# A two-layer kernel's list planner: new step prices, a serial pair and another set of due times for the recurrent layer

## The chip, the core and the metric

The kernel runs on one core of a Trainium2 chip, as one program. The metric is the device time of that program in microseconds (us); a profile of one execution gives a span, from the first to the last instruction, and the order and length of every instruction on the five engines: PE (TensorE matmuls; PEld is its weight loads), DVE (VectorE), ACT (ScalarE), POOL (GpSimd) and SP (SyncE, which here issues the DMAs).

## What is computed

Batch 32, 128 tokens, width 512, all in float32. Layer 0 is a cross-attention block with 32 query heads and 8 key/value heads, followed by a layer norm. Layer 1 is a recurrent block. The change touches only layer 1:

```python
xn = _ln(x, ln1_w, ln1_b)
sx = _token_shift(xn, state[:, i1])
xxx = tanh((xn + sx * maa_x) @ maa_w1).reshape(b, l, 5, 1, 32)
xxx = matmul(xxx, maa_w2).reshape(b, l, 5, E)
x5 = xn[:, :, None] + sx[:, :, None] * (maa_stack + xxx)
w = exp(-exp(time_decay + tanh(x5[:, :, 1] @ decay_w1) @ decay_w2))
r = x5[:, :, 3] @ Wr.T;  k = x5[:, :, 0] @ Wk.T;  v = x5[:, :, 2] @ Wv.T
g = silu(x5[:, :, 4] @ Wg.T)
def step(s, rkvw):                     # 32 heads of 16 x 16 state, 128 steps
    a = k_t[:, :, :, None] * v_t[:, :, None, :]
    out = einsum('bhk,bhkd->bhd', r_t, u * a + s)
    return a + w_t[:, :, :, None] * s, out
att = group_norm(outs) * gn_w + gn_b
x = x + (att * g) @ Wo.T
xn2 = _ln(x, ln2_w, ln2_b); sx2 = _token_shift(xn2, state[:, i0])
rr = sigmoid((xn2 + sx2 * ffn_maa_r) @ ffn_Wr.T)
kk = square(relu((xn2 + sx2 * ffn_maa_k) @ ffn_Wk.T))
x = x + rr * (kk @ ffn_Wv.T)
```

## The kernel before

The 32 sequences go in 16 groups of two, so that a tile of one group has 128 partitions (features) and 256 columns (two sequences of 128 tokens); the width of 512 is four such chunks `c`. For each group layer 1 has three parts.

`front` makes, from the layer norm and the shift (`xn`, `sx`), the five mixed inputs `x5` (a small matmul into a PSUM tile `px`, a DVE operation that takes it in, a POOL addition), then the projections `pk`, `pv`, `pr`, `pg` on PE, their copies or activations on ACT, the product `rk` of r and k on DVE (L742 in the profile; the copy of r from the same PSUM tile is L734 on ACT), the gate `gt` (L761 on ACT, L771 on DVE), and the decay exponents `ew`. v is stored to DRAM (`vd`) so that it can be fetched back spread over partitions.

`recurrence` runs, for each chunk and each quarter `dd`, the state update as a scan along time: SP fetches `kv` (eight DMAs of 128 KB for two quarters, L1316), ACT fills the first column, POOL multiplies by k (L1339), DVE scans (L1355) into the PSUM tile `a`, multiplies by r (L1370), and PE sums over the state (`acc`, L1386). PE also computes `pd` (the term with u, from `rk`) and `pc` (centred outputs).

`tail` normalizes (`pvar`, `rstd`, `pb`), applies the gate, projects (`pwo`), adds to x (`x1c`), and runs the feed-forward part (`pkk`, `pkv`, `prr`), and writes the result. Its two weights `fk` and `fr` (1 MB each) are loaded for every group into one buffer.

None of these steps is written out in program order. Each is handed to a planner by `add`, with its engine, a price in us (`work`), the tiles that it reads and writes, and a due time; the planner (`give_out`) then plays a list schedule and writes out the instructions in the order of that play, so that each engine's queue is fixed when the kernel is built. Layer 0 and the first half of `front` for group 0 are planned by one `Plan`, the rest of layer 1 by a second one (`pl1`). On the chip the engines then run their queues in order and wait for each other by semaphores; a price changes nothing but the order.

The due time of a step is its group's number plus an entry of the table `WHEN0` or `WHEN1`, named by engine and tile. `_turns` first pulls every due time down to just below the earliest one among the steps that depend on it, and sets the order in which the tiles of a tag take their buffers. In `give_out` each engine takes, among its ready steps, the one that could start without delay (under 0.3 us) with the smallest due time:

```python
if s.eng != "SP" and s.due > line[first].due + self.ahead:
    continue
at = free[e]
for s0 in s.before:
    at = max(at, s0.end + (0.0 if s0.eng == e else self.AFTER[s0.eng]))
```

`ahead` is the lookahead in groups: no step may be taken that is due later than the earliest unfinished one by more than that. `AFTER` is the time from one engine's end to another's start. `mode` is the shape in which a PE step uses the array ("full", "rows" for `px`, `pew` and `pb`, "cols" for `acc`, `pdd` and `pvar`, "turn" for transposes); a step in another mode than the one before it costs `SWITCH` more. Prices are formulas: `mm(n, times, share)` for PE, 0.215 us for a pass of 256 columns; `dve(n)` = 0.14 + 1.06 n/1000; `pool_(n)` = 0.08 + 2.3 n/1000; some are literal (2.3 for the scan, 0.48 for the operation at `px`). A fetch of `kv` takes 6.0 us of the wire in the plan, and 3.0 us until it has landed.

Small PSUM tiles share the tag "g" with three buffers; it is exempt from the order of turns (`FREE`). `a` and `acc` have one buffer each in PSUM, `kv` and `ar` three in SBUF.

Of the kernel before, what the change touches and what calls it, by code (L numbers as in the profile page):

```python
# [30 lines left out]
SWITCH = 0.17  # L31
# [43 lines left out]
}  # L75
WHEN1 = {
    "ACT": """
        att 0: 0.4337, att 1: 0.2346, att 2: 0.4481, att 3: 42.2036, ew 0: 11.1338, ew 1: -0.2147, ew 2: 26.1389,
        ew 3: -0.1243, gt 0: 26.2110, gt 2: 2.1890, h0: 0.5241, hd: 0.3002, kk 0: 0.9228, kk 2: 20.4292,
        kv 0 0 0: 25.5890, kv 0 0 1: 21.9376, kv 0 1 0: 6.0558, kv 0 1 1: 0.8322, kv 1 0 0: 6.3560, kv 1 0 1: 29.3594,  # L80
        kv 1 1 0: 9.2616, kv 1 1 1: 25.6198, kv 2 0 0: 43.5542, kv 2 0 1: 7.4919, kv 2 1 0: 8.5948, kv 2 1 1: 43.5152,
        kv 3 0 0: 9.4194, kv 3 0 1: 22.4588, kv 3 1 0: 30.1517, kv 3 1 1: 12.4171, pk 0: 26.3643, pk 2: 24.3430,
        pv 0: 22.5942, pv 2: -0.1385, r 0: 26.3795, r 2: 23.3115, rr 0: 40.0790, rr 1: 27.6728, rstd: 26.0489,
        sq 0: -0.1128, sq 1: 23.3775, sq 2: 36.1033, sq 3: 41.1479, w4 0: 25.5550, w4 1: 21.3052, w4 2: 2.5964,
        w4 3: 27.6773, xnc 0: 8.8046, xnc 1: 1.2163, xnc 2: 4.5961, xnc 3: 10.3705, xnt 0: 37.5160, xnt 1: 36.3160,
        xnt 2: -1.1905, xnt 3: 3.6365, xx 0: 20.5242, xx 1: 34.9847, xx 2: 23.3521, xx 3: 22.4330, yk 0: 41.2808,
        yk 1: 20.7056, yk 2: 23.1054, yk 3: 23.1512, yr 0: 42.3101, yr 1: 3.1488, yr 2: 21.3085, yr 3: 2.7447,
        zc 0: 0.7541, zc 1: 27.0647, zt 0: 0.2936, zt 1: 22.7466
    """,
    "DVE": """  # L90
        a 0 0: 23.1285, a 0 1: 44.6967, a 0 2: 19.4777, a 0 3: 17.2122, a 1 0: 22.0121, a 1 1: 24.8715, a 1 2: 8.6631,
        a 1 3: 9.3222, a 2 0: 23.2268, a 2 1: 8.2943, a 2 2: 21.2763, a 2 3: 8.0300, a 3 0: 1.3330, a 3 1: 44.9810,
        a 3 2: 36.5134, a 3 3: 42.7805, ar 0 0: 1.0179, ar 0 1: 22.3833, ar 0 2: 27.7052, ar 0 3: 25.6817,
        ar 1 0: 37.2615, ar 1 1: 13.6436, ar 1 2: 22.7659, ar 1 3: 45.7511, ar 2 0: 6.0171, ar 2 1: 12.5578,
        ar 2 2: 28.8789, ar 2 3: 15.8516, ar 3 0: 23.3130, ar 3 1: 23.1491, ar 3 2: 19.9556, ar 3 3: 32.9812,
        gn 0: 23.7852, gn 1: 20.9580, gn 2: 33.5535, gn 3: 46.4228, gt 0: -0.0231, gt 2: -0.1977, own 0: 5.1099,
        own 1: 0.1224, own 2: -0.0283, own 3: 0.3349, pb 0: 8.0751, pb 1: 2.2968, pb 2: 0.8375, pb 3: 20.4024,
        raw 0: 23.2010, raw 1: 3.5965, raw 2: 23.2455, raw 3: 44.4584, rk 0: -0.7509, rk 1: -0.1719, rr 0: 1.6746,
        rr 1: 1.3382, rstd: 7.6463, st c 0: 11.1186, st c 1: 40.4898, st t 0: 28.5724, st t 1: 15.0321, x1c 0: 2.5303,
        x1c 1: 26.0962, x5 0 0: 2.7039, x5 0 1: 2.7955, x5 0 2: 24.3069, x5 0 3: 21.8074, x5 1 0: -0.0972,  # L100
        x5 1 1: 21.6197, x5 1 2: 0.6004, x5 1 3: 22.4358, x5 2 0: 42.1808, x5 2 1: -0.8591, x5 2 2: 41.2059,
        x5 2 3: 37.6158, x5 3 0: 26.8334, x5 3 1: 24.0914, x5 3 2: 23.6554, x5 3 3: 2.4313, x5 4 0: 25.8630,
        x5 4 1: 22.1314, x5 4 2: 40.0832, x5 4 3: 41.0197
    """,
    "PE": """
        acc 0: 22.3033, acc 1: 7.0581, acc 2: 22.7806, acc 3: 4.9952, pb 0: 27.7390, pb 2: 22.7260, pc 0: 2.0619,
        pc 1: 28.1521, pc 2: 3.1673, pc 3: 23.4917, pd 0: 33.6053, pd 1: 24.8921, pd 2: 20.8375, pd 3: 23.9500,
        pdd: -1.1093, pew 0: 23.8627, pew 2: 5.8633, pg 0: 23.5794, pg 2: 22.0824, ph0: -0.4813, pk 0: -1.0989,
        pk 2: -0.6925, pkk 0: 19.1077, pkk 2: 22.4386, pkv 0: 19.0064, pkv 1: 23.2658, pr 0: 1.2036, pr 2: 2.3445,
        prr 0: 1.8637, prr 1: 21.7968, pv 0: -0.8518, pv 2: 7.2890, pvar: 5.4151, pwo 0: 32.7897, pwo 1: 23.4460,  # L110
        px5 1 0: 39.8845, px5 1 2: 11.2421, px5 2 0: 23.4434, px5 2 2: 23.3758, px5 4 0: 0.9353, pxnc 0: 24.0019,
        pxnc 2: 21.6438, pxnt 0: -1.1522, pxnt 2: 13.7523
    """,
    "POOL": """
        kv 0 0 0: 26.0772, kv 0 0 1: 23.5502, kv 0 1 0: 27.7860, kv 0 1 1: 29.1526, kv 1 0 0: 0.4056,
        kv 1 0 1: 25.8430, kv 1 1 0: 5.7684, kv 1 1 1: 31.4921, kv 2 0 0: 28.2020, kv 2 0 1: 19.5485,
        kv 2 1 0: 29.7046, kv 2 1 1: 42.4003, kv 3 0 0: 10.6540, kv 3 0 1: 4.0853, kv 3 1 0: 25.5882,
        kv 3 1 1: 22.5557, rr 0: 2.4732, rr 1: 44.9550, sd c 0: 18.3198, sd c 1: 13.1243, sd t 0: 33.5214,
        sd t 1: 22.7124, sxc 0: 2.6017, sxc 2: 21.1060, sxt 0: 21.9776, sxt 2: -1.3154, x5 0 0: 41.1636,
        x5 0 2: 2.6161, x5 1 0: 34.2012, x5 1 2: 22.9652, x5 2 0: 22.8432, x5 2 2: 24.0895, x5 3 0: 23.6407,  # L120
        x5 3 2: 27.8090, x5 4 0: 41.2196, x5 4 2: 26.2718, xx 0: 24.1836, xx 2: 9.4476, yk 0: 24.7724, yk 2: 33.3339,
        yr 0: 1.5862, yr 2: 3.3642
    """,
    "SP": """
        fk: 43.5334, fr: 16.5653, kv 0 0 0: 26.7655, kv 0 1 0: 23.9392, kv 1 0 0: 24.5017, kv 1 1 0: 4.2079,
        kv 2 0 0: 5.4685, kv 2 1 0: 28.7358, kv 3 0 0: 28.1974, kv 3 1 0: 22.0650, rr 0: 3.0366, rr 1: 1.8101,
        s0 0: -0.6787, s0 1: 24.2956, vd 0: 11.0274, vd 1: 0.8056, vd 2: -0.1035, vd 3: 13.7197, x1c 0: 41.2264,
        x1c 1: 2.1599, x1t 0: 23.3682, x1t 1: 35.1410
    """,
}  # L130

# [29 lines left out]
class Plan:  # L161
# [6 lines left out]
    def __init__(self, ctx, tc, when, ahead):  # L168
# [6 lines left out]
                self.when[f"{eng} {name.strip()}"] = float(at)  # L175
        self.pools, self.steps, self.begun, self.turns = {}, [], {}, True

    def tag(self, name, bufs, space=None):
        kw = {} if space is None else {"space": space}
        pool = self.ctx.enter_context(self.tc.tile_pool(name=name, bufs=bufs, **kw))  # L180
        self.pools[name] = (pool, bufs, [])
# [66 lines left out]
    def give_out(self):  # L248
# [95 lines left out]
def xattn_rwkv_kernel(  # L344
# [263 lines left out]
    def front(g, D):  # L608
# [120 lines left out]
        for c in range(0, KC, 2):  # L729
# [5 lines left out]
                r=[pp],  # L735
# [894 lines left out]
```

## Time and profile before

| | us |
|---|---|
| median of 3 runs (lowest, highest) | 2126.89 (2120.77, 2129.71) |
| the profiled execution | 2124.67 |
| its span | 2122.9 |

| engine | busy us | share of the span | instructions |
|---|---|---|---|
| PE | 1975.3 | 93% | 11908 |
| PEld | 1280.5 | 60% | 11908 |
| DVE | 1787.5 | 84% | 2182 |
| ACT | 1048.4 | 49% | 3473 |
| POOL | 1294.3 | 61% | 1081 |

The granted clock of PE over the span is 0.975 on average. A float32 matmul is recorded as two instructions. Matmuls overlap in the records: one of 256 columns has a mean of some 385 ns, while sixteen in a row take 3.65 us; the busy time of PE counts overlapping ones once. Layer 0 ends at about 640 us, the first scan of layer 1 starts at 691 us, and the last ends at 2062.7 us. The columns of every view are named where lines are shown; "idle" is the time in which the engine stood just before an instruction, with what ended it. The kernel's instructions are in a helper's line in some cases (L546 for all projections, L564 for those by token), and the tile's name tells them apart.

### The profile page before, as it was taken

To read this page: it belongs to the slowest core of one execution; us is meant where nothing else is said; L and a number is where in the kernel's file an instruction comes from. 1 tells how busy PE (TensorE), PEld (TensorE's weight loads), DVE (VectorE), ACT (ScalarE), POOL (GpSimd) and SP (SyncE) were. 2 spreads that over 40 slices of the span, in tenths; PEclk is the share of its full clock that TensorE was granted. 3 is DMA by queue.
4 is the path that set the end of the run, shared out by engine and by line. 5 is a ranking of instruction groups with operands and counts; after the bars stand their busy time and mean duration, and the time that the engine had idled before them with its cause. 6 is when DMAs were issued, how large, how long until landed. Compare 5 with 4: busy or idle time off the path is not lost.

```text
span 2122.9 us, 36158 instructions
## 1 busy us (share of the span) xinstructions
PE 1975.3 (93%) x11908; PEld 1280.5 (60%) x11908; DVE 1787.5 (84%) x2182; ACT 1048.4 (49%) x3473; POOL 1294.3 (61%) x1081
## 2 busy tenths in 40 slices
PE   6989999999988689999999999999999999999976
PEld 5656666666656356666566665665656656566533
DVE  3878898988872899989889898998988989989881
ACT  4867888888872133443334434344343443433332
POOL 1363342424245767878678786777867868778652
PEclk9999999999999799999999999999999999999997
DMA  7232222222114887887879879798797887978870
GB/s 203 71 115 63 65 66 65 61 69 62 41 41 91 127 123 124 151 161 125 158 129 152 160 123 162 130 152 161 118 167 127 150 165 120 164 139 128 158 133 30
DMA packets 155947, 252.23 MB, mean 119 GB/s; under 512 B 50576, under 2 KB 97712, under 8 KB 139376
## 3 DMA queue, kind: packets, MB, share of 16 engines
q1 hardware_dynamic: 151136, 242.31, 62.4%
q10 hardware_dynamic: 4624, 7.63, 1.1%
q8 instruction: 94, 1.54, 0.4%
q14 instruction: 93, 0.76, 0.2%
HBM read 224.12 MB, written 25.69 MB: 118 GB/s over the span
## 4 chain that ended last, share of the span: by engine, by line
PE 31%; DMA 16%; DVE 11%; SPq 5%; issue 1%; ACT 1%; POOL 0%; DVEq 0%; POOLq 0%; ACTq 0%
DMA kv<-vd 16%; PE pk L546 5%; PE pkk L546 5%; DVE a L1355 5%; SPq L721 3%; PE pwo L564 3%; PE px L637 3%; PE acc L1386 3%; PE pg L546 2%; DVE ar L1370 2%; PE pv L546 2%; PE pkv L564 2%; SPq L1316 2%; PE pdd L705 1%; PE ph L532 1%
## 5 line engine op out<-in xcount | busy, mean ns | idle before, releaser
L1339 POOL TENSOR_TENSOR kv<-kv,kx 128x1016 f32<-128x1016 f32 x256 | 597.5, 2351 | 164.8 <-DMA kv<-vd 118.7
L1355 DVE TENSOR_TENSOR_SCAN a<-w,kv 128x1024 f32<-128x1024 f32 x256 | 586.7, 2292 | 15.3 <-ACT kv L1329 2.9
L1062 ACT ACTIVATE pr<-pr,mx 128x128 f32<-128x128 f32 x1024 | 396.1, 391 | 51.0 <-DVE mx L1049 38.5
L1370 DVE TENSOR_TENSOR ar<-a,r 128x1024 f32<-128x1024 f32 x256 | 312.4, 1220 | 8.4 <-DVE a L1355 0.5
L668 POOL TENSOR_TENSOR x<-x,xnt 128x512 f32<-128x512 f32 x160 | 186.5, 1184 | 71.0 <-DVE x L653 70.8
L1062 ACT ACTIVATION_READ_ACCUMULATOR pr<-pr,mx 128x1 f32 x1024 | 194.3, 190 | 0.0
L1036 DVE TENSOR_TENSOR pr<-sc,m 128x1024 f32<-128x1024 f32 x128 | 155.9, 1218 | 28.7 <-PE sc L1020 25.0
L1074 PE MATMUL ppT<-ident,pr 128*128 128x128 f32 x1024 | 154.7, 282 | 21.9 <-ACT pr L1062 6.3
L653 DVE SCALAR_TENSOR_TENSOR x<-px,col,sxt 128x256 f32<-128x256 f32 x320 | 134.6, 474 | 36.5 <-PE px L637 34.2
L1386 PE MATMUL acc<-ar,give 128*32 128x256 f32 x2048 | 140.5, 390 | 25.1 <-DVE ar L1370 25.1
L1074 PEld LDWEIGHTS ppT<-ident,pr 128*128 128x128 f32 x1024 | 114.6, 142 | 76.7 <-ACT pr L1062 30.4
L1049 DVE TENSOR_REDUCE mx<-pr 128x8 f32<-128x1024 f32 x128 | 155.0, 1211 | 2.2
L1081 DVE COPY pT<-ppT 128x512 f32<-128x512 f32 x192 | 129.4, 683 | 14.3 <-PE ppT L1074 14.0
L546 PE MATMUL pr<-x,wr 128*128 128x256 f32 x512 | 121.8, 387 | 14.2 <-DVE x L653 13.1
L546 PE MATMUL pk<-x,wk 128*128 128x256 f32 x512 | 125.9, 396 | 3.4 <-ACT kx L685 2.9
L546 PE MATMUL pkk<-yk,fk 128*128 128x256 f32 x512 | 123.1, 389 | 4.9 <-POOL yk L512 4.5
L564 PE MATMUL pwo<-wo,gt 128*128 128x512 f32 x256 | 124.2, 621 | 1.3 <-DVE gt L1468 0.9
L962 PE MATMUL pq<-xT,wq 128*128 128x256 f32 x512 | 123.5, 386 | 0.8 <-ACT xT L913 0.7
L546 PE MATMUL pg<-x,wg 128*128 128x256 f32 x512 | 122.8, 388 | 0.5 <-ACT att L1421 0.4
L546 PE MATMUL pv<-x,wv 128*128 128x256 f32 x512 | 120.1, 383 | 1.2 <-ACT xnt L472 1.2
L564 PE MATMUL prr<-fr,yr 128*128 128x512 f32 x256 | 119.3, 599 | 0.7 <-ACT rr L1529 0.7
L546 PEld LDWEIGHTS pr<-x,wr 128*128 128x128 f32 x512 | 97.5, 193 | 34.7 <-DVE x L653 19.9
(146 smaller groups left out, 3554.6 us busy)
## 6 DMA issues: line engine op xcount, KB each, us to landing
kv<-vd SPq DMA_DIRECT2D x1024, 128.0 KB
fk<-in_fWkT_dram SPq DMA_DIRECT2D x16, 1024.0 KB
fr<-in_fWrT_dram SPq DMA_DIRECT2D x16, 1024.0 KB
x<-in_x_dram SPq DMA_DIRECT2D x32, 256.0 KB
ct<-in_ctxT_dram SPq DMA_DIRECT2D x32, 256.0 KB
bc<-rd SPq DMA_DIRECT2D x256, 32.0 KB
x1d<-z SPq DMA_DIRECT2D x32, 256.0 KB
x1t<-x1d SPq DMA_DIRECT2D x32, 256.0 KB
```

The lines of the kernel that those rows point to most:

```text
L546: nc.tensor.matmul(pp()[:, i], (w() if isinstance(w, Cell) else w)[:, kc, (c + i) * P : (c + i + 1) * P], flat(src()[:, kc]), start=(kc == 0),
L564: nc.tensor.matmul(pp(), src()[:, c, b, :], (w() if isinstance(w, Cell) else w)[:, c, :], start=(c == 0), stop=(c == KC - 1),)
L653: lambda i=i, c=c, pp=pp, half=half: nc.vector.scalar_tensor_tensor(flat(ts[i]()[:, c]), pp()[:, half], col[:, MS0 + i, c : c + 1], flat(s ...
L668: lambda i=i, c2=c2: nc.gpsimd.tensor_add(ts[i]()[:, c2 : c2 + 2].rearrange("p c b t -> p (c b) t"), ts[i]()[:, c2 : c2 + 2].rearrange("p ...
L1036: lambda b=b, sc=sc, jp=jp, pr=pr: nc.vector.tensor_tensor(pr(), sc()[:, 2 * jp : 2 * jp + 2].rearrange("p j g e s -> p (j g e) s"), ms[b] ...
L1049: lambda pr=pr, mx=mx: nc.vector.tensor_reduce(mx(), pr(), AX.X, ALU.max, negate=True),
L1062: nc.scalar.activation(pr()[:, 4 * i + h, :], pr()[:, 4 * i + h, :], AF.Exp, bias=mx()[:, 4 * i + h : 4 * i + h + 1], accum_out=sm()[:, h0 ...
L1074: nc.tensor.transpose(pt()[:, h, :], pr()[:, 4 * i + h, :], ident)
L1339: lambda c=c, kv=kv, e=e: nc.gpsimd.tensor_tensor(kv()[:, e, :, :, 1:T], kv()[:, e, :, :, 1:T], k()[:, c, :, 0 : T - 1].unsqueeze(1).broad ...
L1355: lambda kv=kv, a=a, e=e: nc.vector.tensor_tensor_scan(a().rearrange("p j b t -> p (j b t)"), w4().rearrange("p j b t -> p (j b t)"), kv() ...
L1370: lambda c=c, a=a, ar=ar: nc.vector.tensor_tensor(ar(), a().rearrange("p j b t -> p j (b t)"), flat(r()[:, c]).unsqueeze(1).broadcast_to([ ...
L1386: nc.tensor.matmul(acc()[32 * j : 32 * j + 32, :N], give[:, d].rearrange("p e h -> p (e h)"), tiles[d]()[:, j], start=(d == 0), stop=(d == 3),
```

## The change

The planner of layer 1 gets factors for the prices of an engine (DVE 0.94, POOL 0.97), 0.04 us more for every PE step, 0.1 us instead of 0.17 for a change of shape on PE, and 0.1 us between a DVE step and a DVE step that needs its result. The step that makes `rk` is given the copy of r as one more tile that it reads, so that the planner places it behind that copy; the instruction itself is the same. The lookahead goes from 0.7291 to 6.3924 groups, and every entry of `WHEN1` is replaced (about 260 numbers; a few are shown). The table has one new entry, `pre` of SP, for which this kernel has no step. `WHEN0` and the plan of layer 0 keep their values. The instructions of layer 1 are the same before and after, in another order.

```diff
@@ WHEN1
     "ACT": """
-        att 0: 0.4337, att 1: 0.2346, att 2: 0.4481, att 3: 42.2036, ew 0: 11.1338, ew 1: -0.2147, ew 2: 26.1389,
+        att 0: 9.3544, att 1: 0.4503, att 2: 0.5752, att 3: 2.6316, ew 0: -0.2996, ew 1: 11.8831, ew 2: 0.2128,
...
     "SP": """
...
-        s0 0: -0.6787, s0 1: 24.2956, vd 0: 11.0274, vd 1: 0.8056, vd 2: -0.1035, vd 3: 13.7197, x1c 0: 41.2264,
-        x1c 1: 2.1599, x1t 0: 23.3682, x1t 1: 35.1410
+        s0 0: 5.7680, s0 1: 55.5145, vd 0: 1.6879, vd 1: 7.6463, vd 2: 0.6017, vd 3: 16.0538, x1c 0: 4.0487,
+        x1c 1: 53.1129, x1t 0: -0.3076, x1t 1: 5.4530, pre: -0.9066
...
@@ Plan.__init__
         self.pools, self.steps, self.begun, self.turns = {}, [], {}, True
 
+        self.rate, self.begin, self.switch, self.own = {}, 0.0, SWITCH, 0.0
@@ Plan.add
+        work = work * self.rate.get(eng, 1.0) + (self.begin if eng == "PE" else 0.0)
         s = Step(eng, work, fn, due, mode)
@@ Plan
+    def _after(self, e0, e):
+        if e0 != e:
+            return self.AFTER[e0]
+        return self.own if e == "DVE" else 0.0
@@ Plan.give_out
-                        at = max(at, s0.end + (0.0 if s0.eng == e else self.AFTER[s0.eng]))
+                        at = max(at, s0.end + self._after(s0.eng, e))
...
-            turn = SWITCH if s.eng == "PE" and s.mode != mode else 0.0
+            turn = self.switch if s.eng == "PE" and s.mode != mode else 0.0
@@ xattn_rwkv_kernel
-    pl1 = Plan(ctx, tc, WHEN1, 0.7291)
+    pl1 = Plan(ctx, tc, WHEN1, 6.3924)
@@ front, the step of rk
-                r=[pp, (g.k, c), (g.k, c + 1)],
+                r=[pp, (g.k, c), (g.k, c + 1), (g.r, c)],
                 w=[g.rk[c // 2]],
@@ xattn_rwkv_kernel, before the second plan is filled
     pl = pl1
+    pl.rate, pl.begin, pl.switch, pl.own = {"DVE": 0.94, "POOL": 0.97}, 0.04, 0.1, 0.1
```

More of the change, by code (lines that the diff above doesn't have):

```diff
@@ L77 @@
     "ACT": """
-        att 0: 0.4337, att 1: 0.2346, att 2: 0.4481, att 3: 42.2036, ew 0: 11.1338, ew 1: -0.2147, ew 2: 26.1389,
[L79 to L87, printed above, removed]
@@ L88 @@
-        zc 0: 0.7541, zc 1: 27.0647, zt 0: 0.2936, zt 1: 22.7466
+        att 0: 9.3544, att 1: 0.4503, att 2: 0.5752, att 3: 2.6316, ew 0: -0.2996, ew 1: 11.8831, ew 2: 0.2128,
+        ew 3: 2.9081, gt 0: 8.7561, gt 2: 14.9987, h0: 0.2233, hd: 11.9457, kk 0: 1.3855, kk 2: 2.1483,
+        kv 0 0 0: 6.9788, kv 0 0 1: 22.7468, kv 0 1 0: 3.5957, kv 0 1 1: 1.7056, kv 1 0 0: 20.3165, kv 1 0 1: 8.4565,
+        kv 1 1 0: 6.0351, kv 1 1 1: 15.3716, kv 2 0 0: 1.6738, kv 2 0 1: 2.3053, kv 2 1 0: 61.9582, kv 2 1 1: 6.9921,
@@ new lines @@
+        kv 3 0 0: 27.3250, kv 3 0 1: 13.0129, kv 3 1 0: 16.5636, kv 3 1 1: 10.9667, pk 0: 19.0904, pk 2: 7.0324,
+        pv 0: 3.5277, pv 2: 18.2671, r 0: 10.9880, r 2: 18.9638, rr 0: 57.3359, rr 1: 7.1889, rstd: 7.7805,
+        sq 0: 0.3092, sq 1: 14.0759, sq 2: 2.2363, sq 3: 11.6735, w4 0: 54.7678, w4 1: 2.3093, w4 2: 3.9912,
+        w4 3: 16.8699, xnc 0: 13.2793, xnc 1: 5.7969, xnc 2: 5.8076, xnc 3: 4.8327, xnt 0: 51.5746, xnt 1: 4.8831,
+        xnt 2: -1.3596, xnt 3: -0.2529, xx 0: 7.0607, xx 1: 2.7373, xx 2: 22.6203, xx 3: 3.0888, yk 0: 6.0321,
@@ L89 @@
+        yk 1: 1.2317, yk 2: 17.3009, yk 3: 0.9857, yr 0: 9.7395, yr 1: 7.4822, yr 2: 15.2370, yr 3: 11.9918,
+        zc 0: 0.6963, zc 1: 12.3703, zt 0: 13.2762, zt 1: 3.5163
     """,
     "DVE": """
-        a 0 0: 23.1285, a 0 1: 44.6967, a 0 2: 19.4777, a 0 3: 17.2122, a 1 0: 22.0121, a 1 1: 24.8715, a 1 2: 8.6631,
-        a 1 3: 9.3222, a 2 0: 23.2268, a 2 1: 8.2943, a 2 2: 21.2763, a 2 3: 8.0300, a 3 0: 1.3330, a 3 1: 44.9810,
-        a 3 2: 36.5134, a 3 3: 42.7805, ar 0 0: 1.0179, ar 0 1: 22.3833, ar 0 2: 27.7052, ar 0 3: 25.6817,
@@ L94 @@
[L94 to L103, printed above, removed]
+        a 0 0: 21.5755, a 0 1: 0.4663, a 0 2: 6.4660, a 0 3: 21.7426, a 1 0: 20.0229, a 1 1: 9.6349, a 1 2: 10.9629,
@@ new lines @@
+        a 1 3: 16.5139, a 2 0: 54.2042, a 2 1: 60.8670, a 2 2: 16.2612, a 2 3: 3.1886, a 3 0: 56.3929, a 3 1: 9.1347,
+        a 3 2: 15.6391, a 3 3: 14.2001, ar 0 0: 16.1741, ar 0 1: 15.1052, ar 0 2: 5.3808, ar 0 3: 52.7414,
+        ar 1 0: 11.7517, ar 1 1: 10.7879, ar 1 2: 1.7867, ar 1 3: 15.0146, ar 2 0: 5.9588, ar 2 1: 11.2808,
+        ar 2 2: 23.1563, ar 2 3: 25.0188, ar 3 0: 53.1400, ar 3 1: 4.3907, ar 3 2: 5.9064, ar 3 3: 7.4986,
+        gn 0: 14.4374, gn 1: 18.8217, gn 2: 7.2157, gn 3: 54.0361, gt 0: 0.4226, gt 2: 0.2118, own 0: 22.7830,
@@ new lines @@
+        own 1: 5.0031, own 2: 0.1977, own 3: 3.0090, pb 0: 7.0364, pb 1: 6.3136, pb 2: 1.2765, pb 3: 2.4944,
+        raw 0: 16.1540, raw 1: 0.5659, raw 2: 2.1615, raw 3: 7.9607, rk 0: -0.5490, rk 1: 20.8687, rr 0: 4.8730,
+        rr 1: 10.5798, rstd: 59.6503, st c 0: 15.0328, st c 1: 51.3332, st t 0: 7.2262, st t 1: 8.7387,
+        x1c 0: 10.9782, x1c 1: 13.3288, x5 0 0: 7.7030, x5 0 1: 2.8129, x5 0 2: 7.4244, x5 0 3: 8.9484,
+        x5 1 0: 25.0589, x5 1 1: 7.7630, x5 1 2: 2.4873, x5 1 3: 26.4450, x5 2 0: 1.2832, x5 2 1: 10.3222,
@@ L104 @@
+        x5 2 2: 56.3433, x5 2 3: 11.0440, x5 3 0: 3.9699, x5 3 1: 23.5668, x5 3 2: 56.3776, x5 3 3: 58.0418,
+        x5 4 0: 20.9855, x5 4 1: 9.7484, x5 4 2: 2.2473, x5 4 3: 5.0919
     """,
     "PE": """
-        acc 0: 22.3033, acc 1: 7.0581, acc 2: 22.7806, acc 3: 4.9952, pb 0: 27.7390, pb 2: 22.7260, pc 0: 2.0619,
-        pc 1: 28.1521, pc 2: 3.1673, pc 3: 23.4917, pd 0: 33.6053, pd 1: 24.8921, pd 2: 20.8375, pd 3: 23.9500,
-        pdd: -1.1093, pew 0: 23.8627, pew 2: 5.8633, pg 0: 23.5794, pg 2: 22.0824, ph0: -0.4813, pk 0: -1.0989,
@@ L109 @@
[L109 to L112, printed above, removed]
+        acc 0: 17.5931, acc 1: 9.2014, acc 2: 10.9480, acc 3: 5.3020, pb 0: 1.0080, pb 2: 3.5834, pc 0: 12.7776,
@@ new lines @@
+        pc 1: 21.2693, pc 2: 1.6235, pc 3: 10.9940, pd 0: 10.1011, pd 1: 1.0744, pd 2: 52.4369, pd 3: 3.5976,
+        pdd: -1.1375, pew 0: 5.7651, pew 2: 52.4785, pg 0: 18.5600, pg 2: -0.3099, ph0: 3.6128, pk 0: 9.4502,
+        pk 2: -1.2148, pkk 0: 55.8135, pkk 2: 6.9115, pkv 0: 8.4950, pkv 1: 55.1120, pr 0: 5.4986, pr 2: 2.1467,
+        prr 0: 14.1984, prr 1: 52.9151, pv 0: -0.4623, pv 2: 6.8722, pvar: 7.2237, pwo 0: 8.3667, pwo 1: 57.0309,
+        px5 1 0: 51.3657, px5 1 2: 19.0082, px5 2 0: -0.5247, px5 2 2: 0.0991, px5 4 0: 9.4605, pxnc 0: 1.6938,
@@ L113 @@
+        pxnc 2: 11.4594, pxnt 0: 6.1823, pxnt 2: -0.3125
     """,
     "POOL": """
[L115 to L122, printed above, removed]
+        kv 0 0 0: 5.9903, kv 0 0 1: 14.8718, kv 0 1 0: 11.7519, kv 0 1 1: 13.0551, kv 1 0 0: 5.8554,
+        kv 1 0 1: 17.9843, kv 1 1 0: 22.3723, kv 1 1 1: 22.4921, kv 2 0 0: 2.6064, kv 2 0 1: 2.3883, kv 2 1 0: 4.9876,
@@ new lines @@
+        kv 2 1 1: 8.1918, kv 3 0 0: 7.2874, kv 3 0 1: 7.4828, kv 3 1 0: 60.0451, kv 3 1 1: 7.7010, rr 0: 1.5776,
+        rr 1: 5.0772, sd c 0: 4.9890, sd c 1: 10.4008, sd t 0: 24.6101, sd t 1: 8.1376, sxc 0: 61.1101, sxc 2: 5.7545,
+        sxt 0: -0.5075, sxt 2: 8.8363, x5 0 0: 4.7852, x5 0 2: 22.7818, x5 1 0: 19.4594, x5 1 2: 2.3630,
+        x5 2 0: 0.1884, x5 2 2: 19.1317, x5 3 0: 12.4480, x5 3 2: 24.8578, x5 4 0: 6.0710, x5 4 2: 64.3026,
+        xx 0: 57.5960, xx 2: -0.0202, yk 0: 5.1578, yk 2: 2.3320, yr 0: 7.3078, yr 2: 52.6162
@@ L123 @@
     """,
     "SP": """
-        fk: 43.5334, fr: 16.5653, kv 0 0 0: 26.7655, kv 0 1 0: 23.9392, kv 1 0 0: 24.5017, kv 1 1 0: 4.2079,
-        kv 2 0 0: 5.4685, kv 2 1 0: 28.7358, kv 3 0 0: 28.1974, kv 3 1 0: 22.0650, rr 0: 3.0366, rr 1: 1.8101,
-        s0 0: -0.6787, s0 1: 24.2956, vd 0: 11.0274, vd 1: 0.8056, vd 2: -0.1035, vd 3: 13.7197, x1c 0: 41.2264,
-        x1c 1: 2.1599, x1t 0: 23.3682, x1t 1: 35.1410
+        fk: 16.8251, fr: 56.3055, kv 0 0 0: 1.5731, kv 0 1 0: 13.0995, kv 1 0 0: 2.4603, kv 1 1 0: 1.2907,
@@ L129 @@
+        kv 2 0 0: 8.7997, kv 2 1 0: 4.7371, kv 3 0 0: 8.7567, kv 3 1 0: 56.7564, rr 0: 2.1261, rr 1: 1.5485,
+        s0 0: 5.7680, s0 1: 55.5145, vd 0: 1.6879, vd 1: 7.6463, vd 2: 0.6017, vd 3: 16.0538, x1c 0: 4.0487,
+        x1c 1: 53.1129, x1t 0: -0.3076, x1t 1: 5.4530, pre: -0.9066
     """,
```

## The prediction

> **What bounds the kernel now.** I first read the busy shares over the whole span, then windows, then the waits of the engine that looked fullest, then the order of two engines inside one period, and last the chain.
>
> The recurrent layer repeats. The chain names the output projection (PE pwo L564) at 1140.87, 1228.40, 1316.19 us and so on; from 877.79 to 1929.33 there are 12 such periods, 87.63 us each. Two of them as windows (columns: window and its length, busy us and instruction count of PE, PEld, DVE, ACT, POOL, then granted clock, DMA share, GB/s):
>
> ```profile
> 1140.87:1228.40 87.53, 84.68 (x474) 54.30 (x473) 79.36 (x89) 34.86 (x78) 65.85 (x50) 1.00 0.87 145
> 1228.40:1316.19 87.79, 84.94 (x474) 54.58 (x473) 79.36 (x89) 34.77 (x78) 65.84 (x50) 1.00 0.85 146
> ```
>
> PE is busy 84.7 of 87.5 us, at full clock. DVE comes next at 79.4, the DMA engines at 0.85 to 0.87. The waits of PE over the same two periods, whole list:
>
> ```profile
> PE pr L546 <- DVE x L653: 1.9, 2, 0.9
> PE ph L532 <- DVE x1c L1483: 1.4, 2, 0.7
> PE pb L1452 <- DVE gt L771: 1.4, 2, 0.7
> PE pd L1290 <- DVE gt L771: 1.1, 2, 0.5
> ```
>
> So PE stands 5.8 us in two periods, at the same four places each time. In all four the operation of DVE that it waits for gives nothing that the matmul reads; what it frees is a PSUM tile, so I read each as a wait for one of the three slots of tag "g". One period holds 0.94 (pr), 0.70 (ph), 0.69 (pb) and 0.52 (pd), together 2.85 us. That is what a pure change of order can win in a period without changing PE's own work.
>
> DVE's longest waits in the same window show where its lateness comes from:
>
> ```profile
> DVE rk L742 <- ACT r L734: 2.9, 2, 1.4
> DVE x L653 <- PE px L637: 2.6, 4, 1.1
> DVE rr L1534 <- ACT rr L1529: 2.3, 2, 1.2
> ```
>
> And the timeline ties the first of these to a stall of PE (bracket: idle before, and what ended it):
>
> ```profile
> 1207.61 0.69 DVE L742 TENSOR_TENSOR rk<-pr,kx 128x512 f32<-128x512 f32 x1 [1.45 <-ACT r L734]
> 1208.22 2.29 DVE L1355 TENSOR_TENSOR_SCAN a<-w,kv 128x1024 f32<-128x1024 f32 x1
> 1210.54 1.23 DVE L1370 TENSOR_TENSOR ar<-a,r 128x1024 f32<-128x1024 f32 x1
> 1211.68 1.74 DVE L1445 RECIPROCAL rstd<-rstd 128x256 f32<-128x256 f32 x1
> 1213.34 0.63 DVE L771 SCALAR_TENSOR_TENSOR gt<-gt,pg 128x512 f32<-128x512 f32 x1
> ```
>
> DVE stands 1.45 us for the copy of r, then runs without a gap up to gt at 1213.34, which ends at 1213.97, and PE's pb starts at 1214.03 after 0.69 us idle. Had the product r times k stood one scan later in DVE's queue, gt would have come 1.45 us sooner and pb would not have waited.
>
> For PE's own prices, four pieces of the chain:
>
> ```profile
> 1168.69 1.73 PE pkk L546 x8
> 1170.42 1.06 PE px L637 x8
> 1171.48 1.92 PE pkk L546 x8
> 1173.40 1.00 PE acc L1386 x16
> ```
>
> [...]
>
> **The change part by part.** No instruction is added or removed. The planner writes out the same steps of layer 1 in another order on each queue; layer 0 has its own plan with the old constants, so everything up to about 640 us stays.
>
> *r times k behind the copy.* The trace has the pair serial already: of 27 products, 14 wait for the copy (19.1 us in all), and 12 copies wait for the product (40.7 us on ACT, which is busy 34.8 of 87.5 us). The old plan let both read PSUM at once. The new plan always puts the copy first and knows that the product comes after it. The instruction gains no wait that one of the two has not today. Queued behind the waiting product on DVE are scans and the gate product; behind those waits PE. Gain: the 0.69 us of pb. Bounds: 0 (the product is still put where DVE must wait) to 0.69 per period.
>
> *Works.* For DVE one period's prices add up to 16 scans x 2.30 + 16 products ar x 1.225 + 20 x 0.48 (x) + 12 x 0.411 (own, raw, pb) + 4 x 0.48 (gn) + 1.7 (rstd) + 8 x 0.683 (gt, rk, x1c, rr) + 4 x 1.033 (statistics) = 84.1 us. Measured busy time is 79.36. The old plan thus saw DVE about as full as PE and had to trade one against the other; times 0.94 it is 79.1, and DVE has some 5 us of room in the plan as on the chip. For POOL, 0.97 makes the price of the kv product 2.34 (row: 2.351). Both new prices agree with the rows.
>
> *Own latency, 0.1 us from one DVE step to the next that needs it.* The scan at 1208.22 lasts 2.29 and its dependent starts 0.03 behind its end; an independent step, as the reciprocal at 1211.68, starts 0.09 before its forerunner's end. The difference, 0.1, is the new constant: 16 scans give 1.6 us a period at most. DVE is not the bound, so I book 0, and 1.6 if DVE becomes it. [...]
>
> *Shape change 0.1 for 0.17, and 0.04 for every PE step.* From the chain above: a px visit costs 1.06 against 0.86 of pure streaming (4 x 0.215, the planner's price), and the projection step behind it 1.92 against 1.73, so 0.39 for two changes, 0.2 each. Over a period: 78.3 us of priced matmuls, 84.7 busy, and I count 37 changes of shape in PE's timeline, so 6.4/37 = 0.17 each. The old constant fits better at the margin; the new sum (64 steps x 0.04 + 37 x 0.1 = 6.3) fits as well in total. A search that pays 0.1 for what costs 0.17 to 0.2 will take a few more changes. Between 31 and 43 changes the cost is -1.0 to +1.0 us a period; I take two more, +0.3.
>
> *Due times and lookahead (0.73 to 6.39 groups).* The three other stalls of PE are round trips through a PSUM slot: pg to gt to pd (0.52), px to x to pr (0.94), pwo to x1c to ph (0.70), each with one short step between. One more PE step in between closes each. The wider lookahead makes more steps eligible there, and DVE priced down leaves it freer. Bounds: 0 to 2.16 us gained, or lost as much if new round trips appear; I take half, 1.1.
>
> Each queue is passed by moved steps: SP issues kv fetches in the new order (8 DMAs each, 0.42 us an issue), POOL the kv products. Cover for both: DMA has 0.13 to 0.15 of the period free, about 12 us, POOL 21.7 us. I book 0; without that cover a late fetch costs what the second rival says.
>
> *Start and end.* From 640 to 786 us (first recurrence) and from 2060 us on (last tail, where PE runs in part at half clock and 16 matmuls of pwo take 9.55 us instead of 7.26) the order is changed too. PE idles 8 us in 700:720 alone. A better fill could give 8 us, a worse one take as much; I book 0 and keep +-8.
>
> Sum per period: -0.69 - 1.1 + 0.3 = -1.5 us, so about 86.1. Over 13 periods (the 12 and the one that follows to 2016 us) -19 us. The profiled execution took 2124.67 us with a span of 2122.9; it would become about 2105.5. The median of the runs, 2126.89, is 2.2 above the profiled one, and on it the forecast is 2108 us.
>
> **The rivals.**
>
> *Everything fits (larger gain).* All 2.85 us go, changes of shape stay at 37, start and end give 8: 13 x 2.85 + 8 = 45, so 2082 us. For it: PE then sits at its 84.7 us, and DVE at 80.6 with its gaps still fits under that. Against it: only three slots of "g" for every projection.
>
> *Slower: kv comes late.* The planner prices a kv fetch at 6.0 us on the wire; neither that nor its 3.0 us of landing is changed, while DVE is priced down 5 us. The chain shows what fetches take:
>
> ```profile
> 1190.02 6.01 DMA kv<-vd
> 1196.04 7.38 DMA kv<-vd
> 1203.44 9.87 DMA kv<-vd
> ```
>
> Two of eight fetches a period, each late by the 1.4 to 3.9 us that plan and rows differ, hold POOL's product, the scan behind it and all of DVE: 2.8 to 7.8 us. It decides once more than the DMA engines' 12 us of a period go by unused, or once DVE's idle time of 6.9 us (87.5 less 80.6) is spent. Against the 1.5 gained this nets +1.3 us (2144) up to, with half the upper price reaching PE, +3.4 (2171). For it: over 850 to 2123 us POOL already waits 89.5 us for these fetches. Against it: DVE's scans wait for them hardly at all today (0.4 us in two periods for ACT's copy).
>
> *The change does not do what it says (no change).* PE's work stays and the round trips only move elsewhere: 2.85 us of stalls again, +-0.8 a period, 2116 to 2137. For it: three slots and the chain PE, DVE, PE are untouched.
>
> **How the numbers follow.** Forecast 0.42, larger gain 0.10, no change 0.16, slower 0.32. A measurement of this kernel can tell about 0.5%, 10.6 us, from no change, so the borders are 2116 and 2137: faster 0.52, within 0.16, slower 0.32. The forecast's own range is 2090 to 2116 (stalls taken away between 0.8 and 2.85 us a period). For 8 in 10 I go from 2080 to 2152: what is left out is the end of the larger gain and the upper part of the slower case, about 0.05 and 0.14.
>
> **What would show it.** Right: a period of about 86.1 us in the windows; PE busy still 84 to 85.5; PE's list of waits shorter than 1.8 us a period; no row of r waiting for rk, and rk waiting for r under 0.5 us a period. Shape changes: px and acc in other company, PE's busy time moving by 0.17 for each. Wrong: DVE's scan waiting for POOL or DMA kv by over 1 us a period (second rival); or the four waits replaced by others of the same sum; or the period unchanged and the difference found before 790 or after 2060 us.

## The result and the profile after

The changed kernel takes 2146.55 us (median of 4 runs, 2146.25 to 2147.61); the kernel before, run beside it, 2128.3 (4 runs, 2120.77 to 2130.63). The ratio is 1.0093, with a 95% interval of 1.0067 to 1.0119: slower, where 2108 and faster was forecast. The profiled execution took 2147.61 us, its span is 2145.8 against 2122.9, and the mean granted clock 0.967 against 0.975.

The steady periods of the changed kernel, in the columns of the windows shown above for before:

```profile
1335.73:1423.04 87.31, 85.02 (x474) 54.39 (x473) 79.69 (x90) 34.43 (x78) 65.92 (x50) 1.00 0.83 145
1423.04:1510.34 87.30, 85.01 (x474) 54.39 (x472) 79.69 (x90) 34.32 (x78) 65.89 (x50) 1.00 0.82 148
```

This period is 87.3 us where it was 87.5, PE again the fullest engine. All waits of PE in these two periods:

```profile
PE pk L554 <- DVE gt L779: 2.4, 2, 1.2
PE pd L1299 <- DVE gt L1477: 0.8, 2, 0.4
PE pkk L554 <- DVE own L1307: 0.7, 2, 0.4
PE pwo L572 <- ACT ew L799: 0.6, 2, 0.3
```

pr, ph and pb are gone from the list, but pk, pkk and pwo have come in their place: 2.25 us a period instead of 2.85. And DVE's list of waits over the same two periods:

```profile
DVE a L1364 <- ACT att L1430: 6.2, 2, 3.1
...
DVE a L1364 <- POOL kv L1348: 1.0, 3, 0.3
```

Neither r nor rk is in that list any more, so the pair does what the change says. The scan now stands 3.1 us a period (in the two periods before these it was 4.1 us in all for DMA kv and 3.8 for POOL kv). The profile puts the 3.1 us down to ACT's `att`, which the scan does not read. What it reads is the product of POOL, and the first of the two in this row ends just before the scan starts:

```profile
1397.48 2.33 POOL L676 TENSOR_TENSOR x<-x,xnt 128x512 f32<-128x512 f32 x2 [1.33 <-DVE x L661]
1399.76 4.66 POOL L1348 TENSOR_TENSOR kv<-kv,kx 128x1016 f32<-128x1016 f32 x2
1402.14 2.30 DVE L1364 TENSOR_TENSOR_SCAN a<-w,kv 128x1024 f32<-128x1024 f32 x1 [3.10 <-ACT att L1430]
```

So here the product is late because two additions stand in front of it in POOL's queue, not because a fetch is. No wait of PE in these two periods follows from it: DVE has the room.

So these periods don't hold the loss. I cut each profiled execution at the last matmul record of pwo, group by group. Times in us. "Layer 0" is the start of the last matmul of layer 0's projection `pw`; up to there PE has the same 4420 instructions in the same order in every kernel. "g1" and "g13" are the starts of the last matmul of pwo in groups 1 and 13, twelve periods apart. (The rows with e are the experiments below.)

| kernel | layer 0 | layer 0 to g1 | g1 to g13 | g13 to the end | span |
|---|---|---|---|---|---|
| before | 646.4 | 234.5 | 1051.5 | 190.5 | 2122.9 |
| after | 646.2 | 253.4 | 1053.6 | 192.7 | 2145.8 |
| e1, after with the plan's slots | 643.9 | 238.2 | 1041.3 | 192.4 | 2115.9 |
| e2, before with the plan's slots | 647.7 | 232.2 | 1039.3 | 188.9 | 2108.2 |
| e3, after without the r edge | 650.3 | 241.6 | 1058.6 | 193.6 | 2144.0 |
| e4, before with the r edge alone | 644.8 | 233.6 | 1048.9 | 190.6 | 2117.8 |
| e5, before with the r edge and the plan's slots | 644.9 | 231.8 | 1048.1 | 193.1 | 2117.9 |
| e6, after's own slots in e1's form | 645.8 | 250.9 | 1050.6 | 192.4 | 2139.7 |
| e7, as e6 in the first two groups, then as e1 | 642.4 | 251.3 | 1041.7 | 194.0 | 2129.4 |

Layer 0 ends between 642.4 and 650.3 us although its instructions are the same, so one profile alone does not show differences of a few us in the span. Of the 22.9 us lost, 18.9 lie between layer 0 and g1, in the two groups with which the recurrence starts, and 11.9 of these already before the last pwo of group 0 (789.8 us before, 801.5 after). The twelve periods lose 2.0: nine of them have a mean of 87.5 us against before's 87.6, but three contain a stretch of low clock (3.4 us at 0.50 in each) and take 88.7 to 88.9. The stretch from layer 0 to g1 in both (first row before, second after):

```profile
646.38:880.83 234.45, 202.62 (x1075) 133.51 (x1074) 186.55 (x213) 73.88 (x167) 159.36 (x122) 0.91 0.77 128
```

```profile
646.20:899.58 253.38, 209.88 (x1060) 137.73 (x1058) 182.59 (x210) 73.70 (x167) 153.60 (x120) 0.86 0.73 118
```

PE stands 43.5 us instead of 31.8, and is busy 7.3 us longer, at a granted clock of 0.86 instead of 0.91, with fewer instructions in the stretch (1060 for 1075). What it stands for, in after, from 640 to 896.5 us:

```profile
PE pew L789 <- DVE own L1307: 5.2, 1, 5.2
PE pk L554 <- DVE gt L779: 4.8, 1, 4.8
PE pc L1422 <- DVE x L661: 4.2, 1, 4.2
PE pk L554 <- DVE own L1307: 4.0, 1, 4.0
...
PE pd L1299 <- DVE gt L779: 3.0, 1, 3.0
PE pwo L572 <- DVE gt L1477: 2.9, 1, 2.9
```

In none of these lines does the matmul need what DVE has just made: gt at L779 frees the tile pg, own frees pd, x frees px, gt at L1477 frees pb. (pwo does read gt, but its first matmuls, at 793.59, read the chunks that DVE had written by 788.4.) They are waits for a slot of "g", of 2.9 to 5.2 us each. Before has shorter ones of this kind there (the longest, pk for the copy kx, 2.7 us, is in after too); its largest line is `acc` waiting for the product `ar` (17.1 us in 7), which is data. The timeline shows two of the six and what follows them:

```profile
703.70 5.65 PE L554 MATMUL pk<-x,wk 128*128 128x256 f32 x16 [4.85 <-DVE gt L779]
731.13 5.61 PE L554 MATMUL pk<-x,wk 128*128 128x256 f32 x16 [4.00 <-DVE own L1307]
```

Sixteen records of matmuls of 256 columns take 3.65 us at a clock of 1.00; behind these gaps they take 5.6, at a mean clock of 0.65 and 0.66.

The plan itself has no such waits. By the planner's own times (each with its own prices), the last step of group 0's output projection starts at 126.0 us in after and at 134.8 in before; both plans have a period of 86.9 to 87.0. So all that the new order promised was in the start, and that is where it lost. What I suspected is a mismatch in the kernel: the plan counts a new "g" tile as following the one of the three whose last use ends first in the plan's time, but the slot is chosen by the tile framework, by a rule of its own, when the instructions are written out. Comparing the two for each of the 744 "g" tiles of layer 1, with how late the slot comes free by the plan's times:

```
                        before   after
tiles late by the slot      50      58
after, in the start:  pk 2 of group 1 behind pg of group 0      3.27
                      pk 0 of group 1 behind pd of group 0      3.34
                      pwo of group 0 behind pb                  3.13
                      pew 2 of group 1 behind pd                2.82
                      pd of group 1 behind pg of group 1        2.28
before, a period:     ph behind pwo 1.34, pr behind px 1.24, pb 0.47
```

These are the pairs of the profile's lists, in the start of after and in the steady periods of before. The plan's times are not measurements; the experiments test whether the slot is the cause.

### The profile page after: what moved, and what is told of

It reads as the page before. It is cut to its first block, busy times and chain, and to the rows that moved or that the text cites. A ratio compares the mean times of both kernels' runs of the same rounds, so it can differ in the third digit from the quotient of the medians.

```text
span 2145.8 us, 36250 instructions
## 1 busy us (share of the span) xinstructions
PE 1995.5 (93%) x11908; PEld 1290.8 (60%) x11908; DVE 1792.8 (84%) x2182; ACT 1044.0 (49%) x3473; POOL 1294.5 (60%) x1081
## 4 chain that ended last, share of the span: by engine, by line
PE 49%; DMA 20%; DVE 18%; ACT 4%; POOL 4%; SPq 3%; issue 3%; DVEq 0%; POOLq 0%; ACTq 0%
DMA kv<-vd 13%; DVE a L1364 7%; PE pwo L572 5%; PE pkk L554 5%; PE pw L1135 5%; PE ppT L1082 4%; PE pq L970 4%; DVE ar L1379 4%; PE sc L1028 3%; DMA fk<-in_fWkT_dram 3%; PE pk L554 3%; PE px L645 2%; PE po L1094 2%; PE acc L1395 2%; DMA x1c<-x1d 2%
## 5 line engine op out<-in xcount | busy, mean ns | idle before, releaser
L661 DVE SCALAR_TENSOR_TENSOR x<-px,col,sxt 128x256 f32<-128x256 f32 x320 | 133.4, 475 | 24.3 <-PE px L645 23.9
L572 PE MATMUL pwo<-wo,gt 128*128 128x512 f32 x256 | 129.1, 644 | 7.0 <-ACT ew L799 4.2
L554 PEld LDWEIGHTS pk<-x,wk 128*128 128x128 f32 x512 | 102.6, 204 | 53.9 <-DVE gt L779 21.9
L572 PE MATMUL pkv<-fv,kk 128*128 128x512 f32 x256 | 121.1, 598 | 2.1 <-DVE own L1307 1.7
```

The costliest lines, as they stand in the source:

```text
L554: nc.tensor.matmul(pp()[:, i], (w() if isinstance(w, Cell) else w)[:, kc, (c + i) * P : (c + i + 1) * P], flat(src()[:, kc]), start=(kc == 0),
L572: nc.tensor.matmul(pp(), src()[:, c, b, :], (w() if isinstance(w, Cell) else w)[:, c, :], start=(c == 0), stop=(c == KC - 1),)
```

## The experiments

e1 to e4 ran beside before at 2125.34 us (10 runs), e5 to e8 beside before at 2124.63 (9 runs).

**e1: after with the plan's slots.** The order in every queue stays; the three buffers of "g" become three pools of one buffer each, and each tile of layer 1 takes the pool that the plan counted with. Layer 0 keeps its slots by a written list.

```diff
-        pool = self.ctx.enter_context(self.tc.tile_pool(name=name, bufs=bufs, **kw))
+        if name == "g":
+            pool = [self.ctx.enter_context(self.tc.tile_pool(name=f"g{i}", bufs=1, **kw)) for i in range(bufs)]
...
+    def slot(self, live):
+        if self.given:
+            at = self.given.pop(0)
+        else:
+            at = next(i for i in self.recent if all(o.slot != i for o in live))
...
+                    if c.tag == "g":
+                        c.slot = self.slot(live)
+                        pool = pool[c.slot]
```

> Every queue has the order of the changed kernel; only the PSUM slot of each tile of tag g is different: each slot is a pool of its own in layer 1, so that a tile gets the slot that the planner counted with (layer 0 keeps its slots). Theory A (the start is lost because PE waits for slots that the plan believed free: pk behind gt 4.8 us and behind own 4.0, pew behind own 5.2, pwo behind gt 2.9, and PE's slower clock behind each): these waits go, the first two groups get 15 to 25 us shorter, 2120 to 2131 us. Theory B (the start is lost to kv fetches that come late, 3.3 us behind POOL and 3.4 behind DMA, and to the order of the projections): 2140 us or more, DVE's scans wait as before.

Measured: 2118.81 us (2117.63 to 2122.58), ratio to before 0.997 (0.9957 to 0.9983), 28 us less than the changed kernel (1.2% by the two ratios). In the profile the stretch from layer 0 to g1 falls from 253.4 to 238.2 us, and the period goes from 87.3 to 86.7; its waits of PE over two periods (1052.7 to 1226.1 us):

```profile
PE pk L577 <- DVE gt L802: 2.4, 2, 1.2
PE pwo L595 <- ACT ew L822: 0.6, 2, 0.3
PE pb L1485 <- DVE gt L802: 0.6, 2, 0.3
PE acc L1419 <- DVE ar L1403: 0.4, 2, 0.2
```

pd and pkk are gone, so they were the slot's (pb's 0.3 and acc's 0.2 us are new); pk's 1.2 us stay with the plan's slot, so they are not due to the framework's choice. In the start, too, the 4.2 us of pc stay (5.1 here), while four of the five others of the list are gone; pwo still waits 1.0 us, now in its second half, for data of gt. Three waits of pk have come instead (for ACT's xnt 3.3 us, for DVE's x 2.8, for ACT's att 2.6), so the start is better, not free of waits. PE's busy time in these periods is 84.6 us, that of before, where after had 85.0; pkk and pb, behind the late slots, were busy 0.1 and 0.3 us a period longer there (30.3 us for 30.0 and 7.0 for 5.9 from 1053 to 1400 us).

**e2: before with the plan's slots.** The same edit on the kernel before.

> The kernel before with the same edit: same order in every queue, each tile of tag g in the slot that the planner counted with. Theory A: of PE's four stalls a period three stand at tiles whose slot is not the planned one (pr 0.94, pb 0.69, ph 0.70 us), and go; pd (0.52) stays; a period of 85.3 to 85.8 us, 25 to 30 us less in all, about 2098 to 2104. Theory of the prediction (three slots are too few for these round trips): the stalls stay, 2122 to 2131.

Measured: 2110.63 us (2109.69 to 2111.3), ratio 0.9925 (0.991 to 0.9939): 14.7 us gained, where 25 to 30 were expected. The waits over two periods (1049.1 to 1222.0 us):

```profile
PE pb L1476 <- DVE gt L794: 1.7, 2, 1.1
PE pd L1314 <- DVE gt L794: 1.1, 2, 0.5
PE pg L569 <- ACT att L1445: 1.0, 2, 0.5
```

pr and ph are gone: 1.64 of the 2.85 us a period were the framework's choice of slot. pb, which I expected to go, and pd stay, and pg is new. By its median this is the fastest version measured, 1.7% below the changed kernel. With the plan's slots on both sides the new order is 8.2 us slower than the old one (2118.81 against 2110.63). In the two profiles it loses 6.0 us before g1, 2.0 in the twelve periods and 3.5 behind g13, while e1's layer 0 happened to end 3.9 us earlier.

**e3: after without the r edge**, and **e4: before with the r edge alone** (the same line, put in).

```diff
-                r=[pp, (g.k, c), (g.k, c + 1), (g.r, c)],
+                r=[pp, (g.k, c), (g.k, c + 1)],
```

> The changed kernel without the copy of r among what the product r times k reads, so that the planner takes the two for independent again; prices, due times and lookahead of the changed kernel. If that part is worth what the prediction says: rk waits for r again or r for rk, and a period is 0.7 us longer, 2150 to 2160. If the pair is off the path: the period stays at 87.4 us, and only the start may move, by 10 us either way.

> The kernel before with that one part of the change: the product r times k behind the copy of r in the plan; old prices, due times and lookahead. The prediction books -0.69 us a period for it (pb): about 2118. If DVE's wait is only moved or the stall of pb is one of the slot (theory A): the period stays within 0.3 us of 87.6, 2122 to 2134.

Measured: e3 2145.55 us (2140.37 to 2149.25), ratio 1.0087 (1.0066 to 1.0109), the changed kernel's own time. Its parts differ, though: the start is 11.8 us shorter than the changed kernel's and the twelve periods are 5.0 longer. e4 2114.94 us (2108.69 to 2119.66), ratio 0.9945 (0.9921 to 0.9968): 10.4 us gained. Its waits over two periods (1400.9 to 1575.5 us):

```profile
PE pr L546 <- DVE x L653: 1.9, 2, 0.9
PE pd L1290 <- DVE gt L771: 1.0, 2, 0.5
PE ph L532 <- POOL kv L1339: 0.5, 1, 0.5
PE ph L532 <- DVE x1c L1483: 0.5, 1, 0.5
```

In the old order the edge takes the pb stall away, as booked; PE's waits fall from 2.85 to 2.05 us a period. The size is less certain: the five runs spread over 11 us, and in the profiled one, the slowest, the twelve periods are only 2.6 us shorter. In the new order the edge is worth nothing in total.

**e5: before with the r edge and the plan's slots**, the two gains together.

> Before with the r edge alone and with every g tile of layer 1 in the slot that the plan counted with. Theory A (two separate causes, the slot and r): r took 10 us and the slots took 15 us from before; together about 2100, between 2095 and 2107, with the period at 86.2 to 86.6 and no pb stall left on PE. Theory B (one cause seen twice, PE's stall only moves): no better than the slots alone, 2108 to 2113, with the stall at pb come back at pd, pg or px. At 2118 or more both are wrong.

Measured: 2118.03 us (2111.4 to 2119.68), ratio 0.9961 (0.9947 to 0.9975). Theory A fell: the two gains don't add. Theory B's time is missed too: at 2118 or more both were to count as wrong. Periods of one execution differ, and the windows show how (first a short one, then a long one):

```profile
959.94:1045.66 85.72, 84.54 (x474) 54.51 (x472) 79.36 (x90) 34.77 (x76) 65.80 (x50) 1.00 0.88 146
...
1219.16:1309.12 89.96, 87.44 (x474) 56.16 (x472) 79.64 (x90) 34.78 (x77) 65.90 (x50) 0.98 0.85 141
```

The same instructions keep PE busy 2.9 us longer, at a lower clock (0.98 for 1.00). The timeline of the long one:

```profile
1249.75 0.69 PE L660 MATMUL px<-h,w 32*128 32x256 f32 x2
1251.56 1.30 PE L660 MATMUL px<-h,w 32*128 32x256 f32 x6 [1.11 <-ACT kx L708]
1252.79 3.46 PE L569 MATMUL pkk<-yk,fk 128*128 128x256 f32 x8
```

px waits 1.11 us in the middle of its visit, and the eight matmuls of pkk behind it take 3.46 us instead of the 1.89 that the same eight took at 1247.93, just before it. Four such dips lie between 900 and 2000 us and cost 6.8 us of PE's clock (the sum of 1 less the granted clock, read us by us; none in e2, 1.7 in e4). That is about half of the 12.9 us by which this execution is longer than e2's behind g1; the rest is not explained. One of e5's five executions took 2111.4 us, at a mean clock of 0.970, no higher than the others' 0.970 to 0.972, so the dips are not shown to be the cause. Whether r adds anything to the right slots is open.

**e6: after's own slots in e1's form.** The control of e1: three pools, but a written list of 1140 numbers gives every tile of both layers the slot that the framework gave it in after. Against e1:

```diff
-        pl.given = [int(i) for i in GIVEN]
+        pl.given = pl1.given = [int(i) for i in GIVEN]
```

> A control of e1: the same three single-buffer pools for the g tiles, but each tile in the slot that it has in the changed kernel. Theory A (the slot that a tile lies in made e1's gain): 2143 to 2150, the changed kernel's own time, with the first x8 of pwo near 797 and the period near 87.8. Theory B (e1's gain came from the form with three pools, not from the slots): 2117 to 2125.

**e7: after's slots in the first two groups of layer 1, the plan's from there on.** The list is cut after 106 tiles of layer 1.

> The changed kernel's slots for the first 106 g tiles of layer 1 (about two groups), the plan's slots from there on. Theory A (the start costs 17 of the 28 us between the changed kernel and e1, the steady periods the rest): 2133 to 2140, with g1's pwo near 896 and the period after it near 86.8. Rival (lateness at the start is made up later, and only the steady periods count): 2118 to 2123. Second rival (all of it is the start): 2143 to 2148.

Measured: e6 2140.18 us (2137.89 to 2146.22), ratio 1.0074 (1.0053 to 1.0095); e7 2131.7 (2131.23 to 2134.76), ratio 1.0034 (1.0021 to 1.0047). e6's interval overlaps the changed kernel's, far from e1's, so the slots make the difference and not the form. e6's median is 3 us under the range expected. From e6 to e7 only the steady slots change: 8.5 us, and g1 to g13 falls from 1050.6 to 1041.7. From e7 to e1 only the start's slots change: 12.9 us, and the stretch from layer 0 to g1 falls from 251.3 to 238.2. I had put the start at 17 and measured 13. Lateness of the start is not made up later: e7's periods are those of e1, and it ends later by what it lost.

**e8: matmuls put before a slow group.** In e1 PE still idles 3.29 us before pk 2 of group 1 (first row PE, then ACT):

```profile
700.00 6.32 PE L577 MATMUL pk<-x,wk 128*128 128x256 f32 x16 [3.29 <-ACT xnt L503]
...
698.67 0.31 ACT L1362 COPY kv<-s 128x8 f32<-128x8 f32 x2 [3.13 <-DMA kv<-vd]
698.89 1.01 ACT L503 ACTIVATE xnt<-pxnt,col 128x256 f32<-128x256 f32 x2
```

The edit puts six matmuls of constants ahead of it, into the same tile, overwritten by what follows:

```diff
             def go(i=i):
+                if name == "pk_1_2" and i == 0:
+                    for _ in range(6):
+                        nc.tensor.matmul(pp()[:, 0], w[:, 0, :P], w[:, 0, :N], start=True, stop=True)
                 for kc in range(KC):
```

> e1 with six matmuls of 256 columns more on PE, their result overwritten, ahead of pk 2 of group 1, where PE was idle for 3.29 us and the 16 of pk then took 6.32 us at a granted clock of 0.58. Theory A (the clock is low because PE had been idle): the 16 of pk take 3.6 to 4.2 us at about 0.95 to 1.0, and the whole ends 1 to 3 us sooner than e1. Rival (the clock there has another cause, such as the DMA transfers beside it): pk stays at 5.6 to 6.4 us, and the whole is 0 to 3 us later.

Measured, a single run: 2119.48 us. The six did not fill the gap; they waited for the same thing as pk did (rows below). They read constants alone, so the wait is for the slot, which ACT frees when it has copied pxnt out, and not for data. So the plan's slot can be late as well: in e1 ACT's copy of pxnt stands behind another copy that waited 3.13 us for a fetch of kv (rows above).

```profile
700.93 5.49 PE L578 MATMUL pk<-wk 128*128 128x256 f32 x12 [3.27 <-ACT xnt L503]
706.22 3.73 PE L580 MATMUL pk<-x,wk 128*128 128x256 f32 x16
```

```profile
700.93:706.22 5.29, 5.29 (x13) 4.16 (x14) 5.12 (x5) 0.27 (x2) 3.81 (x3) 0.50 0.67 107
706.22:709.87 3.65, 3.65 (x17) 2.96 (x15) 2.05 (x1) 0.04 (x1) 3.65 (x2) 0.97 0.54 160
```

But they answer the question: twelve records (each matmul is recorded as two) that do nothing for the result run at a clock of 0.50 for 5.3 us, and the same sixteen of pk, now second in line, run in 3.73 us at 0.97. So here the low clock belongs to the first 5.3 us behind the gap, and not to pk. The DMA share is 0.67 and 0.54 in the two stretches, and 0.82 to 0.88 at a clock of 1.00 in the periods above, so transfers don't explain it. The theory's time did not come: no gain, 0.7 us more than e1, from a single run, since the gap was not filled.

## Why the prediction was wrong, point by point

- **What bounds the kernel: right.** In e1 and e2 PE's busy time is 84.4 to 84.7 us a period, as in before, and what moves the periods read here is PE's stalls (2.85 us a period in before, 2.25 in after) and its clock (0.98 for 1.00 in e5's long period).
- **The reading of the four stalls: wrong in two of them, and this is the step behind the rest.** I called all four "a wait for one of the three slots" and took it for granted that a better order would avoid it. e2 removed pr and ph (1.64 us a period) with the order unchanged, by the choice of slot alone. An order that is better by the plan can be worse on the chip, since the plan does not know which slot it gets. pd and pb remained in e2, so they are not the slot's.
- **r times k: right in mechanism for the old order, the size not settled.** Booked 0.69 us a period, 9 us over 13; e4 took pb's stall away and gained 10.4 by its median, but 2.6 us in the twelve periods of its profile. In the new order it is worth nothing in total (e3), and rk waits for r hardly more without it (0.5 us from 900 to 2000 us).
- **Works and own latency:** no experiment separates them from the due times; with only one of the two exchanged the planner finds no place for some step, so no such kernel was run. DVE's busy time stayed (79.36 to 79.69 us a period) and DVE did not become the bound.
- **Shape changes: the sign was wrong, the size small.** I booked two more changes and +0.3 us. Counted over four periods of PE's timeline, there are 33.75 a period instead of 37, and PE's busy time in e1 is that of before (84.6). Measured: about 0.
- **Due times and lookahead: mis-sized.** Booked -1.1 us a period; all parts together gave -0.2 in the two periods shown (87.5 to 87.3) and +0.2 in the mean of twelve (87.6 to 87.8), or -0.8 with the plan's slots (e1). The plan promised no shorter period (86.9 to 87.0 in both). With the new due times the planner writes the same order for a lookahead of 1.5, 3 or 50 groups as for 6.39, and with the old 0.73 it finds no place for some step; so the lookahead has to be wider, but how much is without effect.
- **Start and end: the step that set the sign.** Booked at 0 with +-8, and not worked out. The start cost 18.9 us in the profile and the end 2.2; e6, e7 and e1 give 13 of the 18.9 to the slots. Two terms were missing: a slot of "g" that comes 2.9 to 5.2 us late, and PE's clock behind each such gap (0.50 to 0.58 over the first 3 us in after).
- **Late kv (the slower rival): its wait came, its price did not.** DVE's scan waits 3 to 4 us a period, nearly all of it for kv or POOL's product of it, which was its mark; in the periods read above it is POOL's order that makes the product late. The periods shown did not grow, since DVE's idle time covers the wait (it is busy 79.69 of 87.31 us). The sign was that rival's, the mechanism was not. (Its upper sum was also wrong: half of 7.8 less the 1.5 gained is 2.4 us a period and 2158, not 3.4 and 2171.) In the start a late fetch does reach PE at least once, through ACT's queue (3.13 us of waiting for kv, at e8). What did come is the last of the signs of error: "the period unchanged and the difference found before 790 or after 2060 us"; 11.9 of the 18.9 us lie before group 0's last pwo, at 790 and 801, and the rest before g1.
- **Open:** why the new order is 8.2 us behind the old one even with its own slots. Its plan promised 8.8 us at the end of group 0's projection, yet e1 takes 6.0 us longer than e2 from layer 0 to g1. e1's timeline shows PE behind gaps at a low clock there (6.32 us for pk at 700.00, at 0.57, where the plan counts some 3.6), ACT behind a fetch of kv (3.13 us) and a scan that waits 3.11 us for DMA kv at 720.61; none of them was tested by itself.

## What to carry to other kernels

A static plan is only as good as its picture of the buffers: if another layer picks the slot when the tile is made, let the planner name the slot, or check which tile each wait really stands for. Here that alone was worth 0.75% of the old kernel and 1.2% of the new one. A stall at a buffer says that this buffer was late, not that there are too few of them or that the order is bad; look whether another one was free. And work out the start by itself, besides the period: two groups held most of this loss.

## What the hardware showed

- Gaps cost PE more here than their own length. Behind gaps of 3.3 to 4.9 us (after, e1) sixteen records of matmuls took 5.6 to 6.3 us instead of 3.65, which is 2.0 to 2.7 us more. The clock was 0.50 for the first 5.3 us behind the gap of 3.27 us in e8, and 0.50 to 0.58 over the first 3 us behind each of the six gaps listed for after's start. In the clock records of before and after every stretch of low clock is at 0.50. The stretches last 3.4 us (6 of 14 in before, 15 of 25 in after), 6.8 us (4 and 4) or 10.2 to 23.9 us (3 and 5), but for the last one of each, which the end of the program cuts off.
- A dip also came behind much shorter stops, and not each time. In two periods of the changed kernel the same four matmuls, behind the same 0.30 us of waiting, took 1.98 us and 3.59 (the granted clock is 1.00 from 1676.7 to 1683.7 us and 0.76 from 1764 to 1771):

```profile
1678.27 1.98 PE L572 MATMUL pwo<-wo,gt 128*128 128x512 f32 x4 [0.30 <-ACT ew L799]
...
1765.58 3.59 PE L572 MATMUL pwo<-wo,gt 128*128 128x512 f32 x4 [0.30 <-ACT ew L799]
```

Gaps of 1.1 to 1.5 us before pk, once a period in after, e1 and e7, went by without any dip (sixteen records of pk took 3.72 us behind 1.53 us in after and behind 1.46 in e7), while one followed 1.11 us within px in e5 (a clock of 0.74 from 1251.5 to 1258 us). Both places with a dip lie among matmuls of 32 or 64 rows (px; pew and pb) with stops between them; that this is what counts is a guess that no run tested, and none followed 1.44 us within px in e2, at 1601.4.
- Executions differ where the instructions don't: layer 0's last matmul starts between 642.4 and 650.3 us in the nine profiles of the table. How much of the spread between runs of one kernel (e4: 2108.69 to 2119.66) comes from the dips is not shown; e4's runs of 2108.69 and 2119.2 us have nearly the same mean clock, 0.977 and 0.976.
